# Softmax maxima in the first halves of a causal attention: scores made once, key by query, with the maxima found over transposed blocks and subtracted in SBUF

## The chip, the core and the metric

The kernel runs on one core of a Trainium2 chip. The metric is the device time of one execution in microseconds (us). Five engines work side by side: PE (TensorE, matrix products into PSUM), DVE (VectorE), ACT (ScalarE, copies and functions such as the exponential), POOL (GpSimd) and SP (SyncE, which here issues the DMAs). Each engine has its own program and runs it in order; an instruction that waits for another engine holds up everything behind it on its own engine. What runs next on an engine is thus settled when the program is built.

## The reference

The reference is one transformer block with adaptive layer norms, for `x` of 8 sequences of 1024 tokens with 512 features, all in float32. `cond` is 8 x 512, one row for a sequence.

```
mod = silu(cond) @ Wada + bada;  sh_a, sc_a, gt_a, sh_m, sc_m, gt_m = split(mod, 6)
xm = layernorm(x, g1, be1) * (1 + sc_a) + sh_a
q, k, v = split(xm @ Wqkv)                    # 16 heads of 32
scores = where(causal, q @ k.T * 32 ** -0.5, -inf)
x = x + gt_a * ((softmax(scores) @ v) @ Wproj + bproj)
xm = layernorm(x, g2, be2) * (1 + sc_m) + sh_m
x = x + gt_m * (gelu(xm @ W1 + b1) @ W2 + b2)  # 512 -> 2048 -> 512
```

The softmax subtracts the largest score of each row, that is of each query and head, before the exponential.

## The kernel before

**Blocks and groups.** The tokens are cut into 16 blocks `n` of 512 (`TB`): an even block is the first half of a sequence, an odd one the second. A first half attends to its own 512 keys alone, under a causal mask; a second half attends to the first half's keys and to its own. The 16 heads are taken in 4 groups `g` of 4 heads (`HPG`), since 4 heads of 32 features (`hd`) fill the 128 partitions. A tile of 128 x 4 x 512 float32, four banks of PSUM, holds one score unit: 128 keys or queries by 4 heads by up to 512. There is one such tile (its tag is `st`), one bank `po` for the weighted values, and three banks for the linear products. The four triangular strips of 512, 384, 256 and 128 columns, which the causal mask leaves of a 512 x 512 square, are packed into units by `TRIANGLE = [[0], [1, 3], [2]]`: 512, 384 + 128, and 256 columns. Two groups share the tile of the last, so that a first half has 2.5 units of 512 columns a group.

**Attention before, per group.** The scores are computed twice. First with queries on the partitions (`scores_at_once`, the matmuls of line 1389, into `st`): DVE adds the causal mask to the diagonal squares (1403) and takes the maximum of each row (1406). Where PE would otherwise idle, `scores_by_heads` (1357) does the same head by head in the banks of the linear work. `split_maxima` splits each maximum into three bf16 numbers whose sum it is. `maxima_rows` turns them with identity matmuls (1444), so that queries lie along the free dimension, and ACT copies them to `mrow` (1450). Then `weights_T` computes the scores again with keys on the partitions (1469, into `st`), and PE subtracts the maxima by accumulating a product of minus ones with `mrow` (1481). ACT takes the exponential from PSUM into one of three SBUF tiles `pT` (tags `p0` to `p2`, the list `free_p`, line 1493), and POOL sets to zero what lies above the diagonal (1498). `weigh` multiplies by the values (1521, into `po`), and `add_weights` sums the `pT` tiles of a group on POOL (1594) into the first of them, which gives the sums of the softmax. When a group's last tile is weighed, `finish` turns the sums by matmuls with ones (1539), ACT copies (1545, 1548), DVE inverts (1554) and multiplies (1571), and the quotient takes the place of the queries in `qT`.

**Linear work.** Everything else is linear algebra on PE in lines 201 and 641: projections to k, q and v, the output projection `proj`, transposes of the normalized rows (`xh_m` for the MLP's norm, made on ACT in line 580 or 590), and the MLP up and down. Most of these products use Strassen's scheme, whose sums of weights are formed on chip, stored to DRAM (`kept_qkv_S`, `kept_up_S`, `kept_down_S`) and loaded again by SP's queue.

**The order of the work.** A planner writes the programs of all engines while the kernel is built. `note`, `note_pe` and `note_act` keep a model of when each engine is free (`now`), when each operand is written (`written`) and when each buffer is done with (`left`). The linear steps of a block run as generators; `work` advances the one with the least modelled wait. Before each attention matmul, `step_aside(reads, writes)` does linear work while the operands are not due by the model, and beyond that for as long as linear work is behind its share: `pace` adds to `stream["due"]` in proportion to the attention work just done, at `stream["rate"]`. Jobs for DVE (`add_job`, `run_jobs`), POOL and ACT (`excursion`, `run_excursions`, with a limit on how many) wait in lists until the model finds them ready; `run_jobs(True)` puts out all that wait. When the linear work has nothing left, `linear_wait()` is `NEVER`, and attention is put out without cover.

`attend` runs over the blocks. For each weight unit it puts out `weights_T`, then `maxima_rows`, then the values of the unit before (`close`), and then as many score units of the coming groups as keep the scores about a group ahead. Before it, block 0's first score units are put out as soon as its projections are done, while the start still prepares weights.

## Time and profile before

| | |
|---|---|
| Runs | 3616.52, 3617.55, 3620.1 us (median 3617.55) |
| Span of the profiled execution | 3610.1 us |
| Instructions | 121129 |
| Busy of the span | PE 98%, DVE 58%, POOL 56%, ACT 37% |
| DMA | 430 MB, 119 GB/s on average; SP's queue takes 38.8% of 16 engines' span |
| Score matmuls, query by key (1389), busy | 331.6 us |
| Score matmuls, key by query (1469), busy | 330.9 us |
| Products of the values (1521), busy | 305.8 us |
| Row maxima on DVE (1406), busy | 658.5 us |
| Exponentials (1493), busy | 541.0 us |
| Loads of ACT's function tables ahead of them | 88, 112.9 us |
| Sums of the weights on POOL (1594), busy | 1195.6 us |

The profile comes from one execution, on the only core. Busy times of PE overlap a little, since its matmuls are pipelined: what an instruction costs there is better read from the start of one to the start of the next. In rows in order of time the columns are the start, the duration, the engine, the line, the operation, output and inputs, and the shape; in brackets stand the idle time ahead of it and who ended that. In groups, after the shape and count come the busy time and the mean of one in ns, then the idle time ahead of them and what ended it. In windows the busy time and number of instructions stand for PE, its weight loads, DVE, ACT and POOL, then the clock granted to PE as a share of full speed, then the share of the DMA engines' time and the GB/s. The page also cuts the span into 40 slices of 90 us and gives the busy share and PE's clock in each.

### The profile page before, as it was taken

To read this page: it belongs to the slowest core of one execution; us is meant where nothing else is said; L and a number is where in the kernel's file an instruction comes from. 1 tells how busy PE (TensorE), PEld (TensorE's weight loads), DVE (VectorE), ACT (ScalarE), POOL (GpSimd) and SP (SyncE) were. 2 spreads that over 40 slices of the span, in tenths; PEclk is the share of its full clock that TensorE was granted. 3 is DMA by queue.
4 is the path that set the end of the run, shared out by engine and by line. 5 is a ranking of instruction groups with operands and counts; after the bars stand their busy time and mean duration, and the time that the engine had idled before them with its cause. 6 is when DMAs were issued, how large, how long until landed. Compare 5 with 4: busy or idle time off the path is not lost.

```text
span 3610.1 us, 121129 instructions
## 1 busy us (share of the span) xinstructions
PE 3537.6 (98%) x54821; PEld 1777.0 (49%) x54821; DVE 2078.8 (58%) x2316; ACT 1325.9 (37%) x1388; POOL 2038.3 (56%) x2187
## 2 busy tenths in 40 slices
PE   8999999999999999999999999999999999999999
PEld 5434445445554455544555455454554545545445
DVE  6765675563755547465464655746557455564663
ACT  2335334252433523335243351424524244232421
POOL 3666746665456753666536665456654566544660
PEclk9989999999999999999999999999999999999999
DMA  6633333434343343433434334343343433435334
GB/s 202 220 117 104 109 104 110 127 98 128 112 118 110 104 133 113 133 92 98 133 109 148 91 93 132 105 141 101 99 128 105 139 101 101 124 92 155 90 111 138
DMA packets 307894, 430.35 MB, mean 119 GB/s; under 512 B 25900, under 2 KB 176236, under 8 KB 307380
## 3 DMA queue, kind: packets, MB, share of 16 engines
q1 hardware_dynamic: 307264, 422.56, 38.8%
q8 instruction: 432, 7.08, 0.8%
q14 instruction: 82, 0.67, 0.1%
q10 hardware_dynamic: 116, 0.03, 0.0%
HBM read 394.12 MB, written 28.38 MB: 117 GB/s over the span
## 4 chain that ended last, share of the span: by engine, by line
PE 90%; DVE 4%; POOL 2%; ACT 2%; issue 1%; DMA 0%; SPq 0%; ACTq 0%; DVEq 0%; POOLq 0%
PE bank L201 62%; PE st L1469 8%; PE sc L1389 8%; PE po L1521 7%; DVE mx L1406 2%; PE st L1481 2%; PE bank L641 2%; PE bank L1539 2%; POOL pT L1594 1%; POOL xr L161 1%; ACT pT L1493 1%; DVE hT L1003 0%; PE bank L1444 0%; DVE xr L158 0%; ACT hT L945 0%
## 5 line engine op out<-in xcount | busy, mean ns | idle before, releaser
L1594 POOL TENSOR_TENSOR pT<-pT,pT 128x384 f32<-128x384 f32 (+2 forms) x1266 | 1195.6, 981 | 400.4 <-PE po L1521 211.0
L1493 ACT ACTIVATE pT<-st 128x2048 f32<-128x2048 f32 x288 | 541.0, 1878 | 858.2 <-PE st L1481 826.5
L201 PE MATMUL bank<-w,hT 128*32 128x256 f32 x14336 | 805.6, 381 | 1.0 <-ACT rec L1545 0.9
L1406 DVE TENSOR_REDUCE mx<-sc 128x4 f32<-128x2048 f32 (+3 forms) x380 | 658.5, 1754 | 147.7 <-PE sc L1389 140.6
L201 PEld LDWEIGHTS bank<-w,hT 128*32 128x32 f32 x14336 | 455.2, 110 | 338.4 <-issue 42.7
L201 PE MATMUL bank<-xm_m,w 128*32 128x256 f32 x8192 | 498.3, 381 | 3.1 <-ACT xm_m L651 3.0
L201 PE MATMUL bank<-t_m,w 128*32 128x256 f32 x6144 | 392.2, 381 | 0.4 <-DVE t_m L660 0.4
L1498 POOL TENSOR_SCALAR_AFFINE_SELECT pT<-pT 128x512 f32<-128x512 f32 x256 | 162.1, 651 | 400.4 <-ACT pT L1493 400.4
L201 PEld LDWEIGHTS bank<-xm_m,w 128*32 128x32 f32 x8192 | 254.9, 110 | 229.9 <-issue 62.5
L1389 PE MATMUL sc<-kT,qT 32*128 32x512 f32 (+3 forms) x3040 | 331.6, 524 | 7.6 <-DVE mx L1406 7.0
L1469 PE MATMUL st<-qT,kT 32*128 32x512 f32 (+3 forms) x3072 | 330.9, 523 | 6.7 <-DVE mx L1406 5.0
L1403 DVE TENSOR_TENSOR sc<-sc,mask 128x1024 f32<-128x1024 f32 (+1 forms) x159 | 161.5, 1016 | 278.9 <-PE sc L1389 238.9
L1521 PE MATMUL po<-pT,v 128*32 128x512 f32 (+3 forms) x3072 | 305.8, 493 | 10.2 <-POOL pT L1498 10.2
L201 PEld LDWEIGHTS bank<-t_m,w 128*32 128x32 f32 x6144 | 187.1, 110 | 197.2 <-issue 81.7
L201 PE MATMUL bank<-xm_a,w 128*32 128x256 f32 x3968 | 239.8, 380 | 0.0
L201 PE MATMUL bank<-w,qT 128*32 128x512 f32 x2048 | 237.8, 595 | 0.0
L1554 DVE RECIPROCAL rec<-rec 128x128 f32<-128x128 f32 x256 | 226.0, 919 | 6.0 <-ACT rec L1545 6.0
L1389 PEld LDWEIGHTS sc<-kT,qT 32*128 32x128 f32 x3040 | 130.8, 184 | 175.7 <-ACT pT L1493 81.3
L1469 PEld LDWEIGHTS st<-qT,kT 32*128 32x128 f32 x3072 | 130.1, 184 | 164.4 <-issue 71.6
L1493 ACT ACT_TABLE_LOAD x88 | 112.9, 1283 | 205.8 <-PE st L1481 205.3
L201 PE MATMUL bank<-t_a,w 128*32 128x256 f32 x2944 | 188.5, 380 | 0.0
L193 DVE TENSOR_TENSOR hT<-bank,u_u 128x512 f32<-128x512 f32 x192 | 128.4, 683 | 97.0 <-PE bank L201 96.2
(207 smaller groups left out, 3521.3 us busy)
## 6 DMA issues: line engine op xcount, KB each, us to landing
w<-in_L_cond_W_dram SPq DMA_DIRECT2D x384, 256.0 KB
w<-kept_up_S SPq DMA_DIRECT2D x256, 256.0 KB
w<-kept_down_S SPq DMA_DIRECT2D x256, 256.0 KB
w<-kept_qkv_S SPq DMA_DIRECT2D x180, 256.0 KB
w<-in_L_cond_Wqkv_dram SPq DMA_DIRECT2D x147, 256.0 KB
hat<-in_x_dram SPq DMA_DIRECT2D x64, 256.0 KB
w<-in_L_cond_Wproj_dram SPq DMA_DIRECT2D x64, 256.0 KB
xr<-in_x_dram SPq DMA_DIRECT2D x64, 256.0 KB
```

What stands on the lines that cost most here:

```text
L193: nc.vector.tensor_tensor(out, src, other, op)
L201: nc.tensor.matmul(ps[r, :], lhsT[:, r], rhs, start=start, stop=stop, skip_group_check=True)
L641: nc.tensor.transpose(banks[bank][:, ts(t, P)], got[t][:, ts(c, P)], ident)
L1389: nc.tensor.matmul(sc[:, j, c0 : c0 + w], qTs[n][r, gg, ts(qt, P)], keys_of(n, kh)[r, gg, :w], start=True, stop=True, skip_group_check=True,)
L1403: nc.vector.tensor_tensor(place, place, shape_of.to_broadcast(place.shape), ALU.add)
L1406: nc.vector.tensor_reduce(maxima[n, gg][:, kh, qt, :], sc[:, :, c0 : c0 + w], axis=AX.X, op=ALU.max)
L1469: nc.tensor.matmul(st[:, j, c0 : c0 + w], kT[r, gg, ts(k % NTT, P)], qT[r, gg, TB - w :], start=(c0 == 0), stop=False, skip_group_check=True,)
L1493: nc.scalar.activation(pT[:, :, :used], st[:, :, :used], AF.Exp, scale=scale)
L1498: nc.gpsimd.affine_select(diagonal, diagonal, pattern=[[0, HPG], [1, P]], compare_op=ALU.is_ge, fill=0.0, base=0, channel_multiplier=-1,)
L1521: nc.tensor.matmul(po[r, TB - w :], v[:, k % NTT, g * P + j * hd : g * P + (j + 1) * hd], pT[:, j, c0 : c0 + w], start=(k == 0), stop=last ...
L1554: nc.vector.reciprocal(some, some)
L1594: nc.gpsimd.tensor_tensor(into, into, pT[:, j, c0 : c0 + w], ALU.add)
```

## The change

The change rewrites attention for the first halves (even blocks). Second halves keep the method above.

- The scores are computed once, with keys on the partitions (`first_scores`), in units of 512, 384 + 128 and 256 columns for each group; the last is no longer shared by two groups. ACT copies them from `st` into an SBUF tile `pS` (one of `p0` to `p2`), and POOL fills what lies above the diagonal with -1e30.
- DVE reduces each unit with `apply_transpose`: it takes blocks of 32 x 32, transposes them and takes the maximum along the transposed block's rows, so that a maximum over 32 keys is left for each query. `tops` (128 x 4 x 16) holds these for four strips of 32 partitions; the second and third units go through a tile `some` and a maximum.
- `first_maxima` waits for the three reductions, turns `tops` with four identity matmuls into a linear bank, and takes the largest over the four strips (`best`). `wide` is `best` times `choice`, a constant of zeros and ones, which lays the maxima out as blocks with a single nonzero entry in each column; a product of ones with `wide` (a full unit of 512 columns into `st`) then spreads the maxima over all partitions.
- DVE subtracts `st` from the three `pS` tiles in seven pieces, as jobs; with the last piece of a tile the exponential is put out on ACT, in place.
- `first_values` weighs a tile and adds it to the sums as before. `attend_first` sets the order: for each unit the values of group `g - 1`, then the scores of group `g`; `ahead` puts out score units of the second half that follows.
- `attend` now handles odd blocks alone, its list of score units holds theirs alone, and the start puts out three `first_scores` of block 0 instead of five score units. Lines move by 6 before line 1307 of the old kernel and by 7 between there and `attend`.

```diff
+    tops = const.tile([P, HPG, hd], F32, tag="tops", name="tops")
+    nc.gpsimd.memset(tops, 0.0)
+    choice = const.tile([P, TB // hd], F32, tag="choice", name="choice")
...
-    units = [u for ng in groups for u in score_units(*ng)]
+    seconds = [(n, g) for n, g in groups if blocks[n][1]]
+    units = [u for ng in seconds for u in score_units(*ng)]
...
+    def first_scores(n, g, k):
+        parts = first_units(n, g)[k]
+        used = parts[-1][1] + parts[-1][2]
...
+        step_aside(reads, ["st"])
+        st = ps_st.tile([P, HPG, TB], F32, tag="st", name=f"s1_{n}_{g}_{k}")
+        for i, c0, w, _ in parts:
+            for j in range(HPG):
+                r = slice(j * hd, (j + 1) * hd)
+                nc.tensor.matmul(
+                    st[:, j, c0 : c0 + w], kT[r, g, ts(i, P)], qT[r, g, TB - w :], ...
...
+        slot = free_p.pop(0)
+        pT = pp.tile([P, HPG, TB], F32, tag=f"p{slot}", name=f"pS_{n}_{g}_{k}")
+        nc.scalar.copy(pT[:, :, :used], st[:, :, :used])
+        for _, c0, _, _ in parts:
+            nc.gpsimd.affine_select(diagonal, diagonal, ..., fill=MASKED, ...)
...
+        def reduce():
+            nc.vector.tensor_reduce(
+                top, pT[:, :, :used].rearrange("p j (c x) -> p j c x", x=hd),
+                axis=AX.X, op=ALU.max, apply_transpose=True)
+            for i, c0, w, _ in parts if k else ():
+                nc.vector.tensor_tensor(into, into, top[...], ALU.max)
+        add_job(reduce, [("p", slot)])
...
+    def first_maxima(n, g):
+        until_ready([(n, g, k, "reduced") for k in range(3)])
+        step_aside(["tops"], [BANK])
+        for j in range(HPG):
+            nc.tensor.matmul(banks[bank][r, :P], tops[:, j, :], ident, start=True, stop=True)
+        nc.vector.tensor_reduce(
+            best, banks[bank][:, :P].rearrange("p (a x) -> p x a", x=hd), axis=AX.X, op=ALU.max)
+        run_jobs(True)
+        nc.vector.tensor_tensor(wide, best..., choice..., ALU.mult)
+        step_aside(["top"], ["st"])
+        for j in range(HPG):
+            nc.tensor.matmul(st[:, j, :], ones[r, :], flat[r, :], start=True, stop=True)
...
+        def subtract(k, part, j):
+            nc.vector.tensor_tensor(place, place, st[:, heads, TB - w :], ALU.subtract)
+            if ...:                    # the last piece of unit k
+                nc.scalar.activation(pT[:, :, :used], pT[:, :, :used], AF.Exp, scale=scale)
...
+    def attend_first(n, previous):
+        stream["rate"] = planned_time(n) / mine * (0.7 if n == 0 else 1.0)
...
+        for g in range(NC + 1):
+            for k in range(3):
+                if g:
+                    if k == 0:
+                        first_values(n, g - 1, 0)
+                    if k < 2:
+                        first_values(n, g - 1, k + 1)
+                    else:
+                        finish(n, g - 1)
+                if g < NC:
+                    first_scores(n, g, k)       # but block 0's first group, put out at the start
+                    run_excursions(1)
+                    pace(1500)
...
+            if g < NC:
+                first_maxima(n, g)
+                run_excursions(1)
+                pace(1200)
+                if g >= NC - 2:
+                    ahead(3 if g == NC - 2 else 2)
+            else:
+                ahead(len(units))
+                maxima_rows()
...
     def attend():
...
+            if h == 0:
+                attend_first(n, previous)
+                previous = None
+                continue
```

## The prediction

> **What bounds the kernel now.** I read the page's busy times and chain first, then the groups by form, then the order in time of PE around single steps, and last the windows around PE's few gaps.

> ```profile
> PE 3537.6 (98%) x54821; PEld 1777.0 (49%) x54821; DVE 2078.8 (58%) x2316; ACT 1325.9 (37%) x1388; POOL 2038.3 (56%) x2187
> PE 90%; DVE 4%; POOL 2%; ACT 2%; issue 1%; DMA 0%; SPq 0%; ACTq 0%; DVEq 0%; POOLq 0%
> ```

> PE is busy for 98% of the span and makes 90% of the chain that ended last. Its 72 us without work lie mostly at the start and around 160 to 200 us. So PE time taken away is worth its full length, unless PE then waits. What a step costs on PE is read from starts in order of time:

> ```profile
> 1125.24 1.05 PE L201 MATMUL bank<-xm_a,w 128*32 128x256 f32 x16
> 1126.22 1.14 PE L1389 MATMUL sc<-kT,qT 32*128 32x512 f32 x8
> 1127.29 2.80 PE L201 MATMUL bank<-xm_a,w 128*32 128x256 f32 x48
> ...
> 1158.00 1.14 PE L1469 MATMUL st<-qT,kT 32*128 32x512 f32 x8
> 1158.96 0.39 PE L1481 MATMUL st<-mrow,minus_ones 32*128 32x512 bf16 x4
> 1159.29 1.07 PE L1521 MATMUL po<-pT,v 128*32 128x384 f32 x16
> 1160.29 1.53 PE L641 MATMUL bank<-ident,xh_m 128*128 128x128 f32 x12
> ```

> From start to start a score unit of 512 columns takes 1.07 us, and the `L201` before it 0.98 instead of 0.89 (16 x 34.73 us/624, the steady rate in the chain). The subtraction of the maxima (`L1481`) takes 0.33. The transposes of `xh_m` follow with no gap, because ACT made their input 4 us earlier:

> ```profile
> 1151.87 1.88 ACT L1493 ACTIVATE pT<-st 128x2048 f32<-128x2048 f32 x1
> 1153.64 2.92 ACT L580 ACTIVATE xh_m<-xr,offset_m,rstd_m 128x512 f32<-128x512 f32 x4
> ```

> The prices for the other engines, by form:

> ```profile
> L1406 DVE TENSOR_REDUCE mx<-sc 128x4 f32<-128x2048 f32 x190 | 434.9, 2289 | 144.4 <-PE sc L1389 140.6 <-PE bank L1357 1.0
> L1403 DVE TENSOR_TENSOR sc<-sc,mask 128x1024 f32<-128x1024 f32 x95 | 116.9, 1231 | 175.0 <-PE sc L1389 147.8 <-issue 15.6 <-ACT hat L580 9.5
> L1594 POOL TENSOR_TENSOR pT<-pT,pT 128x384 f32<-128x384 f32 x254 | 249.5, 1016 | 79.5 <-PE po L1521 79.5
> L1594 POOL TENSOR_TENSOR pT<-pT,pT 128x128 f32<-128x128 f32 x254 | 112.7, 479 | 0.0
> ```

> **Step 1, PE in the steady state.** Per group (four heads) of a first half, three things go: 2.5 score units at 1.12 us (1.07 and half of the lengthened neighbour), 2.8; the subtraction for 1280 columns, 0.81; the rows of maxima (`L1444`, 0.22 from start to start), together 3.85 us. The key-by-query scores stay, as `L1628` for `L1469`; their last unit, shared by two groups before, now stands alone (0.05). What comes is the turn (4 matmuls of 128 columns, a quarter of `L1521`'s 0.89, so 0.25) and the spread (a 512-column unit, 1.12). Net 2.43 us. The ends: 1.9 with no cost of changing shape, 3.1 if the busy totals are shared out by columns (331.6 us over 145,920 columns). For blocks 2 to 14, 28 groups, 68 us off (53 to 87). Block 0 is step 4.

> **Step 2, load of the others.** DVE per group: reductions of 5.9 us and masks of 2.5 go. Transposed reductions come (taken at the price of `L1406` per element, two of 2.29 and one of 1.22), three small maxima (0.25 each), `best` 0.28, `wide` 0.9 (512 elements in SBUF cost 0.69 to 1.6 in such rows), and subtractions of 5120 elements at `L1403`'s price, 6.5. Net +5.7 us, 182 over 32 groups: DVE goes to 62% of the span. ACT gains copies (4.8 us a group at `L1493`'s price) and loses `mrow` (0.58) and 26 table loads of 1.28: 40%. POOL loses 31 splits of 1.1. SP issues as many DMAs as before. PE's linear work covers all this at no cost wherever it stands between the links; without that cover it is steps 3 to 5.

> **Step 3, the second group of each later first half.** In the built order the seven blocks 2 to 14 are alike. After the turn come 1.8 us of `L201`, the spread, 3.1 us of `L201`, and then the values of the group, `first_scores` of the next one, and the transposes of the previous block's `xh_m`, with no linear matmul among them: that work waits for `xh_m`. On ACT the four `xh_m` stand behind the three exponentials, and these wait for DVE. With the turn at 0 the spread has landed at 3.3 us. DVE then has two subtractions of 1.23, two of 0.97, one of 0.69, two of 0.69 and two evacuations of 0.69 among them, and ends each third at 6.5, 9.8 and 11.2. ACT's exponentials end at 8.4, 11.8 and 12.8, `xh_m` at 15.7. PE is at the first values at 6.2 and waits until 8.5, works 0.9, waits until 11.9, works 2.6, waits about 1.3 for `xh_m`: 6 us of gaps. Before, those waits were 0.4 us a block (all for `xh_m`, 6.1 over 16). Then the clock:

> ```profile
> 250.31 0.45 PE L641 MATMUL bank<-ident,xh_m 128*128 128x128 f32 x1 [2.04 <-ACT xh_m L580]
> 251.42 2.09 PE L1389 MATMUL sc<-kT,qT 32*128 32x512 f32 x8
> ```
> ```profile
> 245.00:250.00 5.00, 3.27 (x24) 0.87 (x24) 1.34 (x3) 4.87 (x6) 1.10 (x2) 1.00 0.20 58
> 250.00:255.00 5.00, 4.44 (x18) 2.43 (x19) 2.62 (x2) 3.15 (x5) 0.00 (x0) 0.54 0.00 0
> ```

> The third number from the right is the granted clock. After a gap of 2.04 us it fell to 0.54 and a unit took 2.09 us instead of 1.14; the four such gaps of 2.0 to 2.5 us cost 1.4 to 3.4 us each. I take 2.5 for the pair. Step 3 is 8.1 us a block, 57 in all. The ends: 30 (gaps of 4.3 us, no fall) to 80 (two full falls).

> [...]

> **Step 4, block 0.** Before, the linear work of this window ended at about 172 us, and the next, `proj` of block 0, began when its last quotient was made:

> ```profile
> 178.46 0.81 PE L1357 MATMUL bank<-kT,qT 32*128 32x384 f32 x1 [4.49 <-DVE mx L1376]
> 186.90 1.22 PE L1357 MATMUL bank<-kT,qT 32*128 32x512 f32 x1 [3.82 <-DVE mx L1376]
> 198.66 1.72 PE L201 MATMUL bank<-w,qT 128*32 128x512 f32 x12
> ```

> The changed order has no linear matmul from the last scores of group 2 to `proj`: two full chains lie bare. By the rows: inverts, reduction, turn, `wide` and spread 9.4 us; subtractions 6.5; reductions of block 1's scores that stand ahead on DVE 5.0; their last bank, then values, 3.6; POOL's adds, which free the slot for the next copy (4 x 1.016 + 4 x 0.479), 6.0; copy, select, second adds (4 x 0.78), copy, selects, reductions, inverts, third reduction, turn to spread 20.2; subtractions 6.5; block 1's masks and reductions ahead of the last values and ones matmul, with the adds, 13.2; inverts and quotient 6.7. That is 77 us, and some 7 more at half clock (the 180 to 200 us slices show 0.5). It starts at 145 us if the 27 us of attention work that is now behind that point shift everything, but the loads and stores of the weights' sums (56 transfers of 256 KB, 15 of the 30 MB moved between 60 and 210 us) then crowd earlier on SP's queue: I take 152. So `proj` starts at 236, not 198.7: 37 us lost (18 to 56).

> **Step 5, small waits.** The copies of the next scores wait for the adds that free a slot, about 0.5 us twice a block (7); between turn and spread 1.8 us must hold `best`, `wide` and three hand-overs, about 0.2 short (5). Together 12 (0 to 30). At the seam of blocks 14 and 15 a ones matmul, four inverts and the quotient run without linear work: 5 (0 to 10).

> **Sum.** 3610.1 - 68 + 57 + 37 + 12 + 5 = 3653. The median of the runs, 3617.55, lies 7.45 above the span: 3661.

> **Rivals.** *The gain wins (faster).* One mechanism: the bubble of step 3 isn't there, since PE reaches the values after the exponentials. Then -68 + 37 + 12 + 5 gives 3603. It decides below 1.0 us of bubble a block; for it, the planner's linear work fills such gaps elsewhere; against it, none stands between in the order. *The transposed reduction is dear.* No row shows one. At twice the price it adds 5.8 us of DVE per group; 12 to 22 us of linear work stand between last scores and turn, so only block 0 shows it fully (5 us), to 1.2 us in each other group: 3666 to 3700. Below nothing too: at half the price block 0 gains 2. I take the plain row, the nearest. [...] *DMA or DVE bind in the first 200 us*: block 0 beyond its bound, 3680 to 3720. *A draw*: steps 3 and 4 at their low ends of 30 and 18, step 5 at 12 and the gain at 60 come to nothing: 3617. That the change does less than it says is excluded: in the built program `L1444`'s matmuls fall from 1024 to 512 and the scores by half.

> **How the numbers follow.** The forecast, 0.62, spans 3630 to 3695. The dear reduction 0.13, the early binding 0.10, the gain 0.11, the draw 0.04. The range, 3612 to 3706, leaves out most of the gain's case and the top of the two dear ones, 2 in 10. 0.2%, 7 us, is about what a measurement here can tell from no change. Faster 0.11, same 0.04, slower 0.85.

> **What would show it.** PE busy down by some 75 to 100 us, its idle time up from 72 to 180 or more. Seven equal gaps of PE in front of values of `pS`, released by ACT's exponentials, then one in front of `L647`'s `xh_m`, clock below 1 there. `proj` of block 0 starting near 236 us with PE under half busy for the 70 us before. Transposed reductions near 2.3 us. I am wrong if PE shows no gap at those values, or if block 0's stretch is filled.

## The result

The changed kernel takes 3693.4 us in the median of its runs (3692.9 to 3698.3), against 3617.4 for the kernel before: a ratio of 1.0216, 95% interval 1.0201 to 1.0230. It is 76 us slower. The forecast was 3661, 43 us slower, in a range up to 3706: the direction was right and so were most of the places, the size was little more than half.

From the page of the changed kernel, the busy times and the shares of the chain that ended last:

```profile
PE 3528.6 (96%) x53285; PEld 1754.3 (48%) x53285; DVE 2288.5 (62%) x2638; ACT 1410.4 (38%) x1414; POOL 2003.0 (54%) x2051
...
PE 82%; DVE 7%; POOL 5%; ACT 3%; issue 2%; DMA 1%; SPq 0%; ACTq 0%; POOLq 0%; DVEq 0%
```

PE has lost its place as the only bound: 82% of the chain instead of 90%, and idle for 163 us instead of 72. Its busy time fell by 9 us only, because busy time counts a matmul at half clock almost twice as long: the eight of a score unit took 2.09 us there, against 1.14 at full clock.

To see where time went, both traces are cut at the first output projection (`proj`) of each block, which is the same work in both. In each stretch the gaps of PE over 0.15 us are summed, time at half clock outside gaps is counted as half lost, and what remains is PE's own time at full clock, from the start of each matmul to the start of the next. All values are us of the profiled executions (spans 3610.1 and 3692.0).

| stretch | before | after | difference |
|---|---|---|---|
| start to `proj` of block 0 | 198.7 | 239.3 | +40.6 |
| from there: PE's own time | 3363.3 | 3316.6 | -46.7 |
| from there: gaps of PE | 37.3 | 94.4 | +57.1 |
| from there: lost to half clock | 10.9 | 41.7 | +30.8 |

The sum, 81.9 within rounding, is the difference of the spans. It is 6 us more than that of the medians: a span lies about 2 us under its execution's time (3692.0 under 3693.84 us in the changed kernel), and the profiled execution of the kernel before, with 3611.85 us, was one of its faster ones.

The waits of PE from there to the end (us in all, times, longest), first in the changed kernel, then in the kernel before:

```profile
PE po L1528 <- ACT pS L1734: 27.3, 14, 2.2
PE bank L201 <- ACT hT L188: 15.7, 9, 2.2
PE st L1476 <- DVE mx L1413: 15.4, 9, 2.2
```

```profile
PE po L1521 <- POOL pT L1498: 10.2, 6, 2.1
PE sc L1389 <- DVE mx L1406: 7.0, 7, 1.0
PE st L1469 <- DVE mx L1406: 4.8, 6, 1.6
```

The 14 waits for exponentials are two in each of blocks 2 to 14. The two lines under them were in no step of the prediction. Of the nine waits for a reduction (`mx`), six are of 2.2 us, one in each odd block from 3 to 13, and behind each of these six stand 3.4 us at half clock: 23.7 us in all. Block 4 shows the two gaps in order of time, on PE and on ACT:

```profile
972.04 1.91 PE L201 MATMUL bank<-t_a,w 128*32 128x256 f32 x32
976.11 1.08 PE L1528 MATMUL po<-pS,v 128*32 128x512 f32 x8 [2.16 <-ACT pS L1734]
979.09 1.93 PE L1528 MATMUL po<-pS,v 128*32 128x384 f32 x16 [1.90 <-ACT pS L1734]
980.95 2.09 PE L1628 MATMUL s<-qT,kT 32*128 32x512 f32 x8
```

```profile
967.90 1.28 ACT L1734 ACT_TABLE_LOAD   x1
974.14 1.91 ACT L1734 ACTIVATE pS<-pS 128x2048 f32<-128x2048 f32 x1 [4.96 <-DVE pS L1727]
977.13 2.86 ACT L1734 ACTIVATE pS<-pS 128x2048 f32<-128x2048 f32 x2 [1.07 <-DVE pS L1727]
979.89 2.91 ACT L586 ACTIVATE xh_m<-xr,offset_m,rstd_m 128x512 f32<-128x512 f32 x4
```

ACT stands 4.96 us at the first exponential, waiting for DVE's subtraction, with the four `xh_m` that would give PE linear work behind it. In windows, the third number from the right is PE's clock:

```profile
974.00:977.00 3.00, 0.89 (x8) 0.16 (x8) 3.00 (x6) 1.91 (x1) 0.00 (x0) 1.00 0.38 126
977.00:980.00 3.00, 1.10 (x12) 0.40 (x12) 1.23 (x3) 2.87 (x3) 0.89 (x1) 0.50 0.00 0
980.00:984.00 4.00, 4.00 (x29) 0.97 (x21) 0.00 (x0) 2.80 (x4) 4.00 (x7) 0.52 0.00 0
```

From 977.0 to 983.8 us PE runs at half clock. So it goes in six of the seven blocks, for 6.8 us each; in block 2 it is 3.4 us.

The waits for `hT`, a copy of a linear bank, are of one kind too: in seven of the nine (one in each of blocks 2 to 14) ACT makes it behind a copy of scores that waited 3.5 us for POOL, and four GELUs. In the same block, on ACT and then on PE:

```profile
1041.04 1.87 ACT L1639 COPY pS<-s 128x2048 f32<-128x2048 f32 x1 [3.50 <-POOL pS L1601]
1042.80 2.56 ACT L951 ACTIVATE hT<-hT,cols 128x512 f32<-128x512 f32 x4
1045.26 0.56 ACT L188 COPY hT<-bank 128x512 f32<-128x512 f32 x1
```

```profile
1045.88 1.93 PE L201 MATMUL bank<-t_m,w 128*32 128x256 f32 x32 [2.08 <-ACT hT L188]
```

In block 0 the chain that ended last crosses from engine to engine. The part with the second bare chain:

```profile
194.70 2.32 DVE some L1659
...
202.21 0.70 PE bank L1692 x8
...
204.17 2.12 PE m L1714 x8
206.32 5.88 DVE pS L1727 x7
212.20 0.61 DVE mx L1383
...
231.95 0.62 PE bank L1451 x16
...
239.34 0.98 PE bank L201 x5
```

The last line is `proj`, at 239.3 us. Two of the new operations, in groups by form, cost what their rows of before had said or less: the transposed reduction 2.30 us (plain: 2.29), `wide` 0.78.

```profile
L1659 DVE TRANSPOSE_TENSOR_REDUCE tops<-pS 128x64 f32<-128x2048 f32 x32 | 73.7, 2303 | 50.1 <-POOL pS L1643 50.1
L1702 DVE TENSOR_TENSOR wide<-best,choice 128x512 f32<-128x512 f32 x32 | 24.8, 776 | 3.3
```

### The profile page after: what moved, and what is told of

Same layout as the page of the kernel before. It is cut to its first block, busy times and chain, and to the rows that moved or that the text cites. A ratio compares the mean times of both kernels' runs of the same rounds, so it can differ in the third digit from the quotient of the medians.

```text
span 3692.0 us, 118361 instructions
## 1 busy us (share of the span) xinstructions
PE 3528.6 (96%) x53285; PEld 1754.3 (48%) x53285; DVE 2288.5 (62%) x2638; ACT 1410.4 (38%) x1414; POOL 2003.0 (54%) x2051
## 4 chain that ended last, share of the span: by engine, by line
PE 82%; DVE 7%; POOL 5%; ACT 3%; issue 2%; DMA 1%; SPq 0%; ACTq 0%; POOLq 0%; DVEq 0%
PE bank L201 57%; PE po L1528 6%; PE sc L1396 6%; PE st L1476 5%; POOL pT L1601 3%; PE s L1628 2%; POOL pS L1601 2%; PE bank L647 1%; PE bank L1546 1%; DVE pS L1727 1%; PE st L1488 1%; PE m L1714 1%; DVE mx L1413 1%; ACT pT L1500 1%; ACT hT L951 1%
## 5 line engine op out<-in xcount | busy, mean ns | idle before, releaser
L1601 POOL TENSOR_TENSOR pT<-pT,pT 128x512 f32<-128x512 f32 (+1 forms) x882 | 922.2, 1082 | 240.8 <-ACT pT L1500 171.6
L201 PE MATMUL bank<-w,hT 128*32 128x256 f32 x14336 | 818.5, 380 | 6.9 <-DVE hT L1009 5.1
L201 PEld LDWEIGHTS bank<-w,hT 128*32 128x32 f32 x14336 | 458.0, 110 | 354.5 <-issue 60.8
L1500 ACT ACTIVATE pT<-st 128x2048 f32<-128x2048 f32 x208 | 390.6, 1878 | 615.8 <-PE st L1488 495.5
L1413 DVE TENSOR_REDUCE mx<-sc 128x4 f32<-128x2048 f32 (+3 forms) x249 | 465.8, 1886 | 215.9 <-PE sc L1396 212.2
L1601 POOL TENSOR_TENSOR pS<-pS,pS 128x128 f32<-128x128 f32 (+2 forms) x384 | 299.1, 815 | 382.2 <-PE po L1528 284.3
L201 PE MATMUL bank<-xm_m,w 128*32 128x256 f32 x8192 | 500.9, 380 | 0.5
L201 PE MATMUL bank<-t_m,w 128*32 128x256 f32 x6144 | 384.3, 381 | 18.3 <-ACT hT L188 15.4
L201 PEld LDWEIGHTS bank<-xm_m,w 128*32 128x32 f32 x8192 | 256.6, 110 | 214.1 <-issue 48.5
L201 PEld LDWEIGHTS bank<-t_m,w 128*32 128x32 f32 x6144 | 191.8, 110 | 191.2 <-issue 51.4
L1639 ACT COPY pS<-s 128x2048 f32<-128x2048 f32 (+1 forms) x96 | 152.1, 1584 | 321.5 <-POOL pS L1601 266.1
L1476 PE MATMUL st<-qT,kT 32*128 32x512 f32 (+3 forms) x2048 | 243.4, 562 | 19.4 <-DVE mx L1413 15.4
L201 PE MATMUL bank<-xm_a,w 128*32 128x256 f32 x3968 | 247.5, 381 | 0.1
L1396 PE MATMUL sc<-kT,qT 32*128 32x512 f32 (+3 forms) x1992 | 238.6, 555 | 1.2 <-DVE mx L1413 0.7
L201 PE MATMUL bank<-w,qT 128*32 128x512 f32 x2048 | 238.3, 594 | 0.0
L1727 DVE TENSOR_TENSOR pS<-pS,m 128x512 f32<-128x512 f32 (+2 forms) x224 | 192.8, 909 | 36.5 <-PE m L1714 36.5
L1734 ACT ACTIVATE pS<-pS 128x2048 f32<-128x2048 f32 (+1 forms) x96 | 153.3, 1623 | 153.7 <-DVE pS L1727 153.4
L1578 POOL TENSOR_TENSOR qT<-top,rec 128x512 f32<-128x512 f32 x62 | 82.4, 1330 | 193.9 <-DVE rec L1561 193.9
```

The lines of the kernel that those rows point to most:

```text
L201: nc.tensor.matmul(ps[r, :], lhsT[:, r], rhs, start=start, stop=stop, skip_group_check=True)
L1396: nc.tensor.matmul(sc[:, j, c0 : c0 + w], qTs[n][r, gg, ts(qt, P)], keys_of(n, kh)[r, gg, :w], start=True, stop=True, skip_group_check=True,)
L1413: nc.vector.tensor_reduce(maxima[n, gg][:, kh, qt, :], sc[:, :, c0 : c0 + w], axis=AX.X, op=ALU.max)
L1476: nc.tensor.matmul(st[:, j, c0 : c0 + w], kT[r, gg, ts(k % NTT, P)], qT[r, gg, TB - w :], start=(c0 == 0), stop=False, skip_group_check=True,)
L1500: nc.scalar.activation(pT[:, :, :used], st[:, :, :used], AF.Exp, scale=scale)
L1601: nc.gpsimd.tensor_tensor(into, into, pT[:, j, c0 : c0 + w], ALU.add)
```

## The experiments

For runs with some blocks by the old method, the changed kernel keeps both: a set `NEW` names the even blocks that attend by the new method; the others have the old code, with the old order of score units around them. The edits are shown against that version. The ratios of this section are to runs of the kernel before that were made beside each run, with medians of 3614.3 to 3616.2 us. The table has the stretches of all runs, from their profiled executions. "Blocks 2 to 13" is the time from `proj` of block 1 to that of block 13, "14, 15" goes on to `proj` of block 15.

| run | median us | to `proj` 0 | blocks 2 to 13 | of it gaps / half clock | 14, 15 |
|---|---|---|---|---|---|
| before | 3617.4 | 198.7 | 2653.2 | 22.0 / 3.4 | 393.8 |
| changed | 3693.4 | 239.3 | 2683.4 | 68.0 / 28.9 | 406.7 |
| no subtraction | 3596.0 | 198.5 | 2638.4 | 21.6 / 1.7 | 392.3 |
| block 0 old | 3656.3 | 200.3 | 2687.1 | 68.8 / 30.9 | 406.8 |
| only block 0 new | 3660.1 | 239.4 | 2661.5 | 25.8 / 6.8 | 394.0 |
| block 14 old | 3687.1 | 242.1 | 2687.6 | 67.5 / 28.9 | 394.0 |
| `xh_m` first | 3687.4 | 240.3 | 2668.1 | 57.3 / 11.8 | 413.6 |
| `xh_m` first, 0 and 14 old | 3626.7 | 197.8 | 2670.8 | 54.6 / 13.2 | 394.0 |
| the same, exponentials late | 3587.5 | 199.3 | 2629.3 | 29.8 / 0.0 | 394.0 |
| the same, sums first too | 3617.8 | 200.1 | 2658.9 | 49.2 / 11.6 | 394.0 |
| changed, exponentials late | 3666.9 | 239.7 | 2642.8 | 39.0 / 12.8 | 416.5 |
| changed, late and `xh_m` first | 3645.6 | 242.0 | 2619.8 | 26.6 / 0.0 | 412.6 |

### What the subtraction on PE is worth

```diff
 # the kernel before, weights_T
-                    start=(c0 == 0),
-                    stop=False,
+                    start=(c0 == 0 or h == 0),
+                    stop=(h == 0),
...
             row = m_rows[n, gg]
-            for j in range(HPG):
+            for j in range(HPG) if h else ():
```

> The kernel before, without the subtraction of the maxima on PE (line 1481) in the first halves; the maxima are still found and turned, and the softmax is then the same by value but without the safeguard. It measures one term of step 1 by itself. From start to start the subtraction costs 0.81 us a group, 26 us over 32 groups. Theory (part of that is the change of shape after a score unit, which stays on PE when the subtraction goes: the changed kernel's scores cost 0.41 us a group more than the same scores cost before): the scores of line 1469 take 10 to 14 us more from start to start over the span, PE's time falls by 12 to 16 us net, 3601 to 3607. Rival (the subtraction's whole price goes, as step 1 had it): the scores keep their price, 24 to 27 us less, 3590 to 3594.

Measured: 3596.0, ratio 0.9951 (0.9936 to 0.9966). The time lies between the theory's range and the rival's; by the interval it is 12 to 23 us less, so the rival's 24 to 27 are excluded. Over the span, the subtraction's 26.0 us are gone, but the scores of line 1469 take 9.6 us more, just under the theory's 10 to 14; PE's own time falls by 14 us in all, within its 12 to 16. PE at the same place, first in the kernel before, then without the subtraction:

```profile
914.62 1.14 PE L1469 MATMUL st<-qT,kT 32*128 32x512 f32 x8
915.59 0.39 PE L1481 MATMUL st<-mrow,minus_ones 32*128 32x512 bf16 x4
915.91 1.07 PE L1521 MATMUL po<-pT,v 128*32 128x384 f32 x16
```

```profile
911.07 1.14 PE L1469 MATMUL st<-qT,kT 32*128 32x512 f32 x8
912.14 1.07 PE L1521 MATMUL po<-pT,v 128*32 128x384 f32 x16
```

A unit takes 0.97 us to the start of a subtraction, but 1.07 to the start of the values. The pair takes 1.29 with the subtraction and 1.07 without: taking the subtraction away is worth 0.22 us a unit, not the 0.32 that stand between its start and the next. The changed kernel has the same 1.07:

```profile
1031.61 1.14 PE L1628 MATMUL s<-qT,kT 32*128 32x512 f32 x8
1032.68 0.64 PE L1528 MATMUL po<-pS,v 128*32 128x256 f32 x8
```

### Block 0

```diff
-    NEW = set(range(0, NB, 2))
+    NEW = set(range(2, NB, 2))      # block 0 by the old method
```

> The changed kernel, but block 0 attends by the method of before; blocks 2 to 14 by the new one. Theory (step 4: block 0 alone has lost 40.6 us up to the start of its output projection, 239.3 against 198.7 us, and nothing later makes up for it): the projection starts at 196 to 202 us and the whole takes 3648 to 3660. Rival (the early loss is slack that the rest would take anyway, or the cost sits in the blocks after): 3670 to 3695.

Measured: 3656.3 us, 37 less than the changed kernel, with `proj` at 200.3 us. The theory holds. The counterpart is `NEW = {0}`:

> The kernel before, but block 0 alone attends by the new method. Theory (step 4 by itself): its output projection starts at 235 to 243 us and the whole takes 36 to 43 us longer than before, 3653 to 3660. Rival (block 0 is dear only together with the rest of the change): within 10 us of the time before.

Measured: 3660.1 us, ratio 1.0126 (1.0111 to 1.0141), `proj` at 239.4. The rival falls; the time is at the top of the theory's range, and the 46 us more than the runs beside it are above its 36 to 43. In the profiled executions 40.7 of the 47.5 us more lie ahead of `proj`. The other 7 lie mostly in blocks 2 to 5; they were not expected, and their cause was not followed. So the new method costs block 0 about 40 us whatever the rest does, and nothing later gives it back.

### The seam after the last first half

```diff
-    NEW = set(range(0, NB, 2))
+    NEW = set(range(0, NB - 2, 2))  # block 14 by the old method
```

> The changed kernel, but block 14 attends by the method of before. Theory (the seam of blocks 14 and 15, where the last first half ends, costs far more than the 5 us of the prediction): in the changed kernel's trace the two stretches between the output projections of blocks 13, 14 and 15 take 406.7 us against 393.8 before, 12.9 more, and 19 us of the first is PE idle or at half clock. With the old method there, 12 to 18 us less, 3675 to 3682. Rival (the seam costs 5 us or less and the rest is the work that the planner moved from one block to the next): 3686 to 3695.

Measured: 3687.1 us, 6 less; the time fell in the rival's range. By stretches, 12.7 us go in blocks 14 and 15, as the theory said, but 4.1 come back in block 13's, which must now hold block 14's first scores and maxima, and block 0's was 2.8 us longer in that execution though nothing was edited there. The seam is worth some 8.6 us to this kernel. The theory took the fall in blocks 14 and 15 for the whole and left out what moves ahead of them.

### What stands behind the exponentials

```diff
             if g < NC:
                 first_maxima(n, g)
-                run_excursions(1)
+                run_excursions(2)
```

> The changed kernel, with two excursions of ACT put out after each turn of the maxima instead of one, so that the four normalized rows (xh_m) of the second group stand ahead of the three exponentials on ACT and no longer behind them. Theory (the bubble of step 3 is linear work locked up behind the exponentials): the changed kernel's profile shows seven times a gap of 2.16 and one of 1.2 to 1.9 us at the values of the second group, 27 us in all, and seven stretches of 3.4 to 6.8 us at half clock behind them, some 20 us lost. With xh_m early, its 16 transposes (2.2 us) and products fill most of this: 30 to 47 us less, 3646 to 3663. Rival (the gaps are the subtractions on DVE themselves, and nothing else is at hand to fill them): the seven gaps stay within 0.5 us, 3685 to 3700. Second rival (the work is only taken from a later place, which then waits): gaps go here and come back elsewhere, 3680 to 3700.

Measured: 3687.4 us, 6 less than the changed kernel: in neither the theory's range nor within its reasons, and the second rival comes nearest. The bubble itself closed. PE in block 8, and ACT there:

```profile
1857.33 0.33 PE L647 MATMUL bank<-ident,xh_m 128*128 128x128 f32 x1
...
1863.55 1.04 PE L1529 MATMUL po<-pS,v 128*32 128x512 f32 x8
...
1872.18 1.05 PE L1529 MATMUL po<-pS,v 128*32 128x384 f32 x16
...
1889.15 3.46 PE L201 MATMUL bank<-xm_m,w 128*32 128x256 f32 x32 [2.51 <-ACT rec L1553]
```

```profile
1856.03 2.94 ACT L586 ACTIVATE xh_m<-xr,offset_m,rstd_m 128x512 f32<-128x512 f32 x4 [2.54 <-DVE offset_m L572]
...
1882.89 1.87 ACT L1640 COPY pS<-s 128x2048 f32<-128x2048 f32 x1 [1.76 <-POOL pS L1602]
1884.78 1.28 ACT L951 ACT_TABLE_LOAD   x1
1886.07 2.56 ACT L951 ACTIVATE hT<-hT,cols 128x512 f32<-128x512 f32 x4
1888.54 0.56 ACT L1553 COPY rec<-bank 128x512 f32<-128x512 f32 x1
```

The `xh_m` run in ACT's idle stretch, PE transposes them, and no gap is left at the values. Yet 26 us later PE waits 2.51 us for a copy of the sums (`rec`), which stands behind a score copy that waited for POOL and four GELUs with their table load. In blocks 2 to 13 gaps fell by 10.7 us and clock losses by 17.1, but PE's own time rose by 12.5, and the seam took 6.9 us more. So a closed gap was paid back in part by new ones. The rise of PE's own time was not settled. From `proj` of block 0 to the end it is 14 us, and 7 of them are matmuls with ones, which in the odd blocks came one by one while POOL finished the sums they read, a wait that this way of counting does not show as a gap.

### The edits together, and exponentials put out late

The three edits in one kernel (`NEW = set(range(2, NB - 2, 2))` and two excursions):

> The three edits so far together: two excursions after each turn, blocks 0 and 14 by the old method. Theory (the three losses lie in different places, so they add up): 6 for the excursions, 37 for block 0, 12 to 18 for block 14, from 3693: 3632 to 3638. Rival (they share a cause): over 3645.

Measured: 3626.7 us, ratio 1.0031 (1.0019 to 1.0044), lower than the sum. With `xh_m` first, the seam had cost 19.6 us (413.6 against 394.0), more than in the changed kernel, which fits what taking it out gave. Then only the moment was moved at which an exponential is put into ACT's program:

```diff
+    exps = []
+
     def until_ready(keys):
         while not weights_ready.issuperset(keys):
+            if exps and (linear_wait() == NEVER or due([exps[0][1]]) <= now["PE"] + 300):
+                exps.pop(0)[0]()
+                continue
...
-                nc.scalar.activation(pT[:, :, :used], pT[:, :, :used], AF.Exp, scale=scale)
-                note_act(170 + 3.34 * used, "exp", [("p", slot)], [("p", slot)])
-                weights_ready.add((n, g, k))
...
+                def exponential():
+                    nc.scalar.activation(pT[:, :, :used], pT[:, :, :used], AF.Exp, scale=scale)
+                    note_act(170 + 3.34 * used, "exp", [("p", slot)], [("p", slot)])
+                    weights_ready.add((n, g, k))
+
+                exps.append((exponential, ("p", slot)))
```

> As the run with the three edits, but an exponential is put out on ACT only when its subtraction is due by the planner's model or nothing else is left, and no longer together with the last piece of the subtraction. Theory (what the new method costs in blocks 2 to 12 is ACT standing at an exponential that waits for DVE, with copies of the linear work behind it, which PE then waits for): ACT's waits for the subtractions, 153 us over the changed kernel, fall by more than half over the same blocks, and the time falls by 8 to 25 us against that run. Rival (ACT's waiting costs nothing, since its copies wait for PE or DVE anyway): within 5 us of it.

Measured: 3587.5 us (3585.3 to 3589.2), 39 less than the run before it, more than was expected, and faster than the kernel before: 0.9922 (0.9907 to 0.9936). ACT's waits for the subtractions, first without and then with late exponentials:

```profile
ACT pS L1735 <- DVE pS L1728: 192.3, 42, 18.8
```

```profile
ACT pS L1743 <- DVE pS L1733: 39.3, 8, 5.9
```

From 192 to 39 us; PE's waits for the copies of the sums fell from 15.9 to 8.0. In blocks 2 to 13 gaps went from 54.6 to 29.8 us, and no time at half clock is left. Its page shows PE as busy as in the kernel before, with 33 us less to do:

```profile
PE 3504.9 (98%) x53669; PEld 1744.8 (49%) x53669; DVE 2265.1 (63%) x2569; ACT 1378.9 (38%) x1403; POOL 2000.2 (56%) x2064
```

Not all of this can be put down to ACT's waits alone, since the planner laid out the odd blocks anew as well; their waits for POOL's masks (17.4 us over the run in the former, 6.5 in the latter) went down too. As to the order of the sums:

```diff
                     if k < 2:
                         first_values(n, g - 1, k + 1)
-                    else:
+                    if k == 1:
                         finish(n, g - 1)
```

> As the run with late exponentials, and the sums and copies that end a group (finish) are put out before the second score unit of the next group instead of after it, so that ACT's copy of the sums (rec) no longer stands behind a copy of scores that waits for POOL to free its slot. In the run with the excursions alone PE waited in each later first half 2.5 us for that copy of the sums, and lost some 1.7 more to the clock in most. Theory (that order is the cause): these gaps go, 12 to 30 us less than the run with late exponentials alone, and the whole comes to 3590 to 3618, level with the kernel before or faster. Rival (PE then waits for POOL's adds at the ones matmuls instead, which come earlier): same time within 5 us, or slower.

Measured: 3617.8 us, ratio 1.0003 (0.9994 to 1.0013), 30 slower than late exponentials alone, where the theory had 12 to 30 less. The waits for `rec` in the even blocks are gone, as the theory said, but the odd blocks 3 to 11 got 7 to 9 us longer, with new waits of up to 1.8 us:

```profile
PE sc L1397 <- DVE mx L1414: 11.5, 7, 1.8
PE st L1477 <- ACT pT L1501: 10.4, 6, 1.8
```

The rival had the outcome, and its place in part. In the third group of each even block from 2 to 12 the eight matmuls with ones take 2.3 us from the first's start to what follows, instead of 0.86: at 1001.58 us the first starts while POOL's four last adds for that group run from 998.09 to 1002.87, and the others come as these end. That is 8.7 us in the six blocks, and no gap shows it. Yet these even blocks got 2.3 us shorter all the same, so the loss lies in the odd ones. It may be that linear work done in an even block is missing in the odd one; how the planner came to these places was not followed.

### Late exponentials alone, and with all first halves new

> The changed kernel, all first halves by the new method, with one edit: an exponential is put out on ACT only when its subtraction is due by the planner's model or nothing else is left. The four xh_m of the second group then stand behind the first exponential, ahead of the second and third. Theory (late exponentials help because other work of ACT, xh_m above all, gets ahead of them; where xh_m still stands behind the first, the first gap of 2.16 us at the values stays and only the later ones shrink): the gaps at the values of the second group fall from 27 us to 10 to 20, and the whole is 5 to 25 us less than the changed kernel, 3668 to 3688. Rival (the lateness by itself is what gave the 39 us between the third and the fourth of the combined runs, whatever stands where): 35 us or more less, under 3658.

Measured: 3666.9 us, 27 less than the changed kernel, a little under the range; the rival's 35 or more are not reached. The gaps at the values fell from 27.3 to 15.1 us, within the 10 to 20. PE and ACT in block 4:

```profile
969.90 1.76 PE L1529 MATMUL po<-pS,v 128*32 128x512 f32 x8 [2.15 <-ACT pS L1742]
971.60 0.90 PE L647 MATMUL bank<-ident,xh_m 128*128 128x128 f32 x3
```

```profile
967.94 1.91 ACT L1742 ACTIVATE pS<-pS 128x2048 f32<-128x2048 f32 x1 [4.96 <-DVE pS L1733]
969.76 2.92 ACT L586 ACTIVATE xh_m<-xr,offset_m,rstd_m 128x512 f32<-128x512 f32 x4
972.58 1.90 ACT L1742 ACTIVATE pS<-pS 128x2048 f32<-128x2048 f32 x1
```

As expected, the first gap stays to 0.01 us, because `xh_m` still stands behind the first exponential; the second is closed.

> Both edits of ACT's order (late exponentials, two excursions after each turn), with all eight first halves by the new method, blocks 0 and 14 too. Theory (block 0's bare chain is one of latency and not of ACT's order, so it stays at 37 to 43 us, and block 14's seam at 6 to 20): against 3587 with blocks 0 and 14 by the old method it is 43 to 63 us more, 3630 to 3650, and the output projection of block 0 starts at 236 to 243 us. Rival (late exponentials cure block 0 as well): the projection starts before 220 us and the whole is under 3617.

Measured: 3645.6 us, ratio 1.0081 (1.0066 to 1.0096), `proj` of block 0 at 242.0. The theory holds: ACT's order does nothing for block 0, whose chain has no linear work to put in. In blocks 2 to 13 this kernel is 33 us faster than the kernel before and 64 faster than the changed one, with the same method: there the loss went with the order in which ACT's work is put out.

## Why the prediction was right, and where its sizes were wrong

- **Step 1, PE's gain: -68 forecast, -46.7 measured, outside its ends of 53 to 87.** This is one of the two failed terms. The query-by-key scores gave back 74.4 us (2.66 a group, 2.8 forecast), and turn and spread cost 0.22 and 1.07 (0.25 and 1.12). But "the key-by-query scores stay" at their price was wrong: `L1628` costs 0.41 us a group more than `L1469` did. The run without the subtraction shows 0.30 of this: the same unit takes 0.97 us up to a subtraction and 1.07 up to the values. Why the one follows sooner than the other is not shown. The rows of maxima gave 0.08 a group, not 0.22, and other neighbours cost 0.2 more.
- **Step 2, the transposed reduction at the plain price: right**, 2.30 us against 2.29. With it falls the rival of a dear reduction: over 128 x 2048 elements the two differ by 14 ns.
- **Step 3, the bubble: +57 forecast, +46 measured**, at two of the three places named. The first gap was 2.16 us (2.3 forecast), the second 1.2 to 1.9 (2.5). The third, in front of `xh_m` (1.3), did not come: its transposes start without a gap in all seven blocks, and only 5 to 7 us after their start PE waits for `t_m`, 2.7 us in six blocks together, 0.7 at most. The seven pairs come to 27.3 us of gaps, and the half clock behind them to 18.2. That the clock would fall was taken from the row of a 2.04 us gap; it fell in all seven. The row alone did not assure that: from `proj` of block 0 on the kernel before has seven gaps of 2.0 to 2.5 us, not four, and behind two of 2.06 us (ending at 2138.55 and 2580.14) the clock stayed full.
- **Step 4, block 0: `proj` at 236 forecast, 239.3 measured**, +40.6 against +37. Right in its total, and both runs on block 0 bear it out. The bare chain starts at 155.2 us (152 forecast). From there to the end of the second subtractions, at 212.2, each link is within about 2 us of its forecast, and the sum 57.0 against 57.2. The last two, 19.9 in the forecast, took 27.1: the last quotient was made at 235.3, but on PE `proj` stood behind more of block 1's scores, 4 us longer, which the forecast did not have there. The 7 us for half clock, which had been put on top, cover the difference, which is luck. PE was busy for 41.7 of the 70 us before `proj`, not for under half, at a mean clock of 0.64. "DMA or DVE bind in the first 200 us" did not come about as a loss beyond the bound, though loads stand in the chain that ended last from 131.8 to 148.0 us.
- **Step 5 and the seam: 17 forecast, 42 measured.** This is the other failed term. It counted the copies of scores that wait for POOL, but not what stands behind them on ACT: copies of linear banks (`hT`), for which PE waits 15.7 us, twice the 7 forecast for all such copies. It had no term for the odd blocks, where PE waits for a reduction, 15.4 us against 4.8 before, with another 10.2 lost to the clock behind six of these waits. Why the reductions come late there was not followed; that work moved out of the odd blocks is a guess. The seam took about 9 us instead of 5.
- **The sum.** From 43 forecast to 82 by the spans: 21 from step 1, -11 from step 3, 4 from step 4 and 25 from step 5. The forecast of PE's busy time, 75 to 100 us less, failed too (9), since it forgot that half clock counts as busy, and so did the idle time, 163 us instead of 180 or more. The step from span to median, 7.45 us, was mostly the difference between two executions. The rivals of a gain and of a draw fell: the bubble was there. The time, at the top of the forecast's own 3630 to 3695, lies in the ranges of both dear rivals too; the rows decide against these, not the time.

## What to carry to other kernels

The price of an operation from its start to the next one's start belonged to the pair here: when the subtraction went, 0.10 of its 0.32 us stayed. Before an engine's in-order program is given an instruction that waits on a long chain, list what is queued behind it and who waits for that; here the same method took 3626.7 us or 3587.5 by the moment at which an exponential was put out. A change that takes work off the bound engine must also be asked, at the ends of the pipeline, what linear work is left to cover its longer chain; where there is none, keep the old method, as the fastest run here does for blocks 0 and 14.

## What was not expected of the hardware

In blocks 2 to 13 of the two kernels PE's clock went to half for 3.4 or 6.8 us at a time and for no other length, behind gaps of about 2 us or more. But a gap of that size did not always do it: in block 4 of the changed kernel the pair of 2.16 and 1.90 us cost 6.8 us at half clock, while a single gap of 2.08 us 67 us later cost none, nor did one of 3.24 us that ended at 1759.96.

```profile
973.61:977.02 3.41, 1.25 (x16) 0.16 (x8) 3.41 (x6) 1.91 (x1) 0.00 (x0) 1.00 0.44 143
1041.88:1045.29 3.41, 1.93 (x24) 0.57 (x16) 1.06 (x1) 3.41 (x6) 1.23 (x2) 1.00 0.44 147
```

The gap of 2.16 us lay whole in the first, and half clock began at 977.02. The gap of 2.08 was divided, 1.49 us in the second and 0.59 in the next, and that of 3.24 into 1.96 and 1.28. Over blocks 2 to 13 of the two traces, a step at full clock with 2.06 us or more of idle time was always followed by half clock, one with 1.88 or less never, and between the two it went either way. The pairs of the changed kernel put 2.15 to 2.35 us into one step in every block, and none escaped. A single gap near 2 us cost itself and, by where it fell, sometimes half of 3.4 us more: of the four of 2.06 us in the kernel before, those ending at 1693.89 and 3021.74 did, those ending at 2138.55 and 2580.14 did not.
